# Dealing the depthwise-convolution steps of the last two images evenly over bands, with the convolution's rows at every second SBUF partition

## The chip, the cores and the metric

The kernel runs on one core of one Trainium2 chip. The metric is the device time of one execution in microseconds (us). The kernel before takes 3230.07 us, the median of three runs from 3227.74 to 3243.27 us.

## The reference

The input is a batch of four images of 128 channels and 128 x 128 pixels, float32. Layer 0 cuts each image into 9 x 9 overlapping regions of 16 x 16 pixels (step 14), runs four-head attention with a layer norm in each region, merges the regions, applies a second layer norm and a projection to 256 channels, a depthwise 5 x 5 convolution, a batch norm over the whole batch, GELU twice, a projection back to 128 channels and a residual. Layer 1 is two quantised 3 x 3 convolutions with batch norms. Cut to the part that the change touches:

```python
xf = merged.transpose(0, 2, 3, 1).reshape(b, h * w, c)
y = _ln(xf, ln2_g, ln2_b)
y = y @ w_p0 + b_p0
ym = y.transpose(0, 2, 1).reshape(b, HIDDEN, h, w)          # 256 channels
ym = jax.lax.conv_general_dilated(ym, dw_k, window_strides=(1, 1), padding=[(2, 2), (2, 2)],
        feature_group_count=HIDDEN, dimension_numbers=('NCHW', 'OIHW', 'NCHW'))
mu = ym.mean(axis=(0, 2, 3), keepdims=True)                  # over all four images
```

## The kernel before, in words

**Bands.** The attention part runs over 36 bands, t = 0 to 35: four images of nine bands, each band a row of nine regions. For every region the order on PE, ACT, DVE and SP is the order in which the program is written (a manual schedule); POOL's order is left to the compiler's planner. `beside(t)` (L931) returns, for each of a band's nine regions, the side work that is issued between the attention steps: layer norm and projections of a later band (`ln1_chunks`), the finish of the band before (`post_chunks`), and steps from the list `todo`, mostly steps of the depthwise convolution. `run` (L990) runs a step and then issues the stores it left (`flush`, L440), all on SP.

**Layer norms.** Each band has four layer-norm chunks. A chunk writes its reciprocal deviations to DRAM (`row`, on ACT's queue) and reads them back spread over 128 partitions (`xn<-row`, L420, on SP's queue); DVE's multiply at L430 waits for that.

**The depthwise convolution.** `post_chunks` stores the 256-channel rows to DRAM (`y2_d`, L440) with pixels of even and odd columns apart, in runs of 64 numbers (256 bytes). For images 0 to 2 they lie in [32 rows (16 image rows, even and odd), 256 channels, 9 groups, 64], so that for one row and four channels everything is one run of 8960 bytes. A convolution step loads 32 such rows and 8 halo rows for each of two groups of channels (`half` 0 and 1) into a tile `u`, half 0 at partitions 0 to 39 and half 1 at 64 to 103, and multiplies it with a banded weight tile `w` (`depthwise`, L613, matmuls at L622 of 40 rows by 32 columns). ACT copies the two results to `c` (L690), DVE takes their statistics (L694) and SP stores them to `cv_d`. `conv_steps(n)` (L636) makes these steps: one `begin` and 32 steps for each of images 0 to 2, one `begin` and 16 steps for the first half (rows 0 to 63) of image 3. A step first issues the loads of the step two ahead.

**Loads of a step.** For images 0 to 2 (L656) there are four: for each half the 32 rows and the 8 halo rows, half 0 on SP's queue, half 1 on ACT's. Image 3 has another layout (`input_of`, L628) and its loads are all on SP (L669). Weight tiles are read from `dw_d` (`weights`, L606), two DMAs of 40 partitions by 3 runs of 1 KB, once for two steps (images 0 to 2) or once for each (image 3). `u` and `w` come from a pool of three buffers each, `c` from a pool `cp` of three.

**Dealing.** Steps of image b are put on `todo` when band t = 9(b + 1) + 1 begins and are dealt over nine bands for images 0 and 1 (three or four in a band), over five bands (t = 28 to 32: 6, 7, 7, 7 and 6) for image 2. The first half of image 3 is put there at t = 33 with a divisor of seven: 2, 3 and 3 steps in bands 33 to 35, and nine steps are left for the tail.

**The tail.** After band 35, `beside(T)` finishes the last band's rows with the nine left steps between its pieces (in the tail they use the score banks of PSUM, and their copies are issued one step late, `pending`). Then `conv_rest` (L734) does the second half of image 3 in 16 steps with tiles of its own, `ur` and `wr`, six of each, loaded by SP and POOL (L746, L608); its results go through the same three `c` buffers (L769) and out in two stores for each half (L776, half 0 on SP, half 1 on ACT).

**Preparation.** In bands 0 to 9 `todo` holds the quantisation of two weights and `band_matrices` (L213), which writes zeros around `y2_d` (`edge`, L232, on SP), builds banded weights in DRAM (`band_d`, L254) and turns them into `dw_d`.

After the tail come the GELU stage (L1234) and the two 3 x 3 convolutions.

Of the kernel before, what the change touches and what calls it, by code (L numbers as in the profile page):

```python
# [48 lines left out]
def layers(  # L49
# [44 lines left out]
    cv_d = [dram.tile([P // GR, 2 * P, GR * P], F32, name=f"cv_d{b}") for b in range(B)]  # L94

    dw_d = dram.tile([2 * NCK, KD, 3, 16 * 32], F32, name="dw_d")
# [88 lines left out]
    with ExitStack() as actx:  # L185
# [8 lines left out]
        up, cp = pool("up", 3), pool("cp", 3)  # L194
# [10 lines left out]

        stores = []
        xb, xr, yr, qs, kr, ob = {}, {}, {}, {}, {}, {}

        def scratch(n):

            return up.tile([P, UW], F32, name="u")[:, :n]

        def band_matrices():  # L213
# [18 lines left out]
            def edge(b, m, n, g):  # L232
                if b == B - 1:
                    d = y2_d[b][P + 2 :] if g else y2_d[b][0:2]
                    out = d.rearrange("r e c x -> (r e c x)").rearrange("(p n x) -> p n x", p=P, x=CW)
                else:
                    out = bass.AP(
                        y2_d[b].tensor, y2_d[b][m, 0, g, 0:1].offset,
                        [[n * NG * CW, P], [NG * CW, n], [1, CW]],
                    )  # L240
                nc.sync.dma_start(
                    out=out, in_=held["zero"][:, : n * CW].rearrange("p (n x) -> p n x", x=CW)
                )
# [26 lines left out]
            def turn(c, s, half):  # L270
# [7 lines left out]
                if half:  # L278
                    del held[c, s]
                    nc.sync.dma_start(  # L280
                        out=dw_d[c // 16 : (c + 64) // 16, :, s, :].rearrange("k p n -> p k n"),
                        in_=by_c.rearrange("p (k n) -> p k n", n=16 * 32),
                    )
# [15 lines left out]

            for n, p in enumerate(pieces):  # L300
# [3 lines left out]
                steps.append(lambda p=p: turn(*p, 1))  # L304
            return steps
# [300 lines left out]
        def weights(wt, k, jj, n, dma):  # L606
            for half in range(2):
                dma(  # L608
                    out=wt[64 * half : 64 * half + KD].rearrange("p s c m -> p s (c m)"),
                    in_=dw_d[2 * k + half, :, :, 256 * jj : 256 * (jj + n)],  # L610
                )

        def depthwise(outs, wt, ut, n):  # L613

            for j in range(n // 4):

                for s, (a, z) in ((1, (0, CW)), (0, (1, CW)), (2, (0, CW - 1))):
                    for half in range(2):
                        hs = slice(64 * half, 64 * half + KD)
# [15 lines left out]

        def conv_steps(n, ahead=2):  # L636
# [8 lines left out]
            def load(at):  # L645
                k, jj, c = tiles[at]
                if c == 0:
                    W[k, jj] = up.tile([P, 3, 8, 32], F32, name="w")
                    weights(W[k, jj], k, jj, 1, nc.sync.dma_start)
                if b < B - 1:  # L650
                    t = scratch(UW)
                    U[at] = bass.AP(t.tensor, t.offset, [t.ap[0], [CW, ng], [NG * CW, nc_], [1, CW]])
                    for a, z in ((0, GR), (GR, GR + 4)):
                        for half, engine in enumerate((nc.sync, nc.scalar)):
                            src = y2_d[b][0, 32 * k + 16 * half + 8 * jj + c, 0, 0:1].offset
                            engine.dma_start(  # L656
                                out=t[64 * half + 2 * a : 64 * half + 2 * z],
                                in_=bass.AP(
                                    y2_d[b].tensor, src + (CW if a else 0),
                                    [[2 * P * NG * CW, 2 * (z - a)], [1, UW]],  # L660
                                ),
                            )
# [3 lines left out]
                for half in range(2):  # L666
                    ch = 32 * k + 16 * half + 8 * jj + c
                    for a, z in ((0, GR), (GR, GR + 4)):
                        nc.sync.dma_start(  # L669
                            out=ut[64 * half + 2 * a : 64 * half + 2 * z].rearrange(  # L670
                                "p g c x -> p g (c x)"
                            ),
                            in_=input_of(b, g0, ng, ch, nc_, a, z),
                        )

            def products(at):
                k, jj, c0 = tiles[at]
                ut, wt = U.pop(at), W[k, jj]
                if tail:
                    pc = score_banks(at, ng)  # L680
                else:
                    pc = [ps_m.tile([P, nj, ng, CW], F32, name="pm") for _ in range(2)]
                depthwise(pc, wt[:, :, c0:], ut, nc_)
                return pc

            def results(at, pc):
                k, jj, c0 = tiles[at]
                for half in range(2):
# [4 lines left out]
                    for j in range(nj):  # L693
# [3 lines left out]
                        ch = 32 * k + 16 * half + 8 * jj + c0 + 4 * j  # L697
                        store(
                            bass.AP(
                                cv_d[b].tensor,  # L700
                                cv_d[b][g0, ch, 0:1].offset,
                                [[CW, P], [2 * P * GR * P, ng], [1, CW]],
                            ),
                            cv[:, j],
                        )
# [6 lines left out]
            for at in range(len(tiles)):  # L712
                def one(at=at):
                    if at + ahead < len(tiles):
                        load(at + ahead)
                    while pending:
                        pending.pop(0)()
                    pc = products(at)
                    if tail:
                        pending.append(lambda: results(at, pc))  # L720
                    else:
                        results(at, pc)
# [11 lines left out]
        def conv_rest(n, pool):  # L734
# [8 lines left out]
            def load(at, a, z, g, m):  # L743
                k, jj = tiles[at]
                for half, engine in enumerate((nc.sync, nc.gpsimd)):
                    engine.dma_start(  # L746
                        out=U[at][64 * half + 2 * a : 64 * half + 2 * z, g : g + m].rearrange(
                            "p g c x -> p g (c x)"
                        ),
# [3 lines left out]
            def begin(at):  # L753
                U[at] = pool.tile([P, ng, 8, CW], F32, name="ur", bufs=ahead)
                W[at] = pool.tile([P, 3, 8, 32], F32, name="wr", bufs=ahead)
                weights(W[at], *tiles[at], 1, nc.gpsimd.dma_start)
# [6 lines left out]
            def step(at):  # L763
# [3 lines left out]
                for half in range(2):  # L767
                    cv = cp.tile([P, 2, ng, CW], F32, name="c")
# [3 lines left out]
                    for j in range(2):  # L772
# [3 lines left out]
                        (nc.sync, nc.scalar)[half].dma_start(  # L776
                            out=bass.AP(
                                cv_d[b].tensor,
                                cv_d[b][g0, 32 * k + 16 * half + 8 * jj + 4 * j, 0:1].offset,
                                [[CW, P], [2 * P * GR * P, ng], [1, CW]],  # L780
                            ),
                            in_=cv[:, j],
                        )
# [147 lines left out]
        def beside(t, sel=None):  # L931
# [7 lines left out]
            if t >= 2:  # L939
                b, i = bands[t - 2]  # L940
                if i == NR - 1 and b < B - 1:
                    todo.extend(conv_steps(b))
                    share[0] = NR if b < B - 2 else 5
                elif b == B - 1 and i == 4:
                    todo.extend(conv_steps(B - 1))
                    share[0] = 7
# [3 lines left out]
            conv = [todo.pop(0) for _ in range(n if t < T else 0)]  # L950
# [3 lines left out]
            if t == T:  # L954
                more = lambda n: [todo.pop(0) for _ in range(min(n, len(todo)))]
                return [
                    *more(2), *b1[:2], *b2[:2], b1[2], *more(1), b1[3], b2[2], *more(1), b2[3], b1[4], b2[4],
                    *more(1), b1[5], b2[5], *more(1), b1[6], *b1[7:], b2[6], *more(1), *b2[7:], *more(len(todo)),
# [39 lines left out]
        todo, share, left, early, tail, pending = [], [0], [], [], [], []  # L998
# [14 lines left out]
        with nullcontext() if safe else tc.manual_schedule(engines=MANUAL):  # L1013
# [30 lines left out]
            tail.append(True)  # L1044
# [5 lines left out]
            run(pending)  # L1050
# [183 lines left out]
    def gelu_stage():  # L1234
        with (
# [7 lines left out]
            def load(n):  # L1243
                b, k = units[n]
                cv = ld.tile([P, 2, U], F32, name="cv")
                nc.sync.dma_start(
                    out=cv,
                    in_=cv_d[b][k // 2].rearrange("(h p) n -> p h n", p=P)[:, :, pixels(k % 2)],
                )
# [204 lines left out]
```

## Time and profile before

| | us |
|---|---|
| median of 3 runs | 3230.07 |
| profiled execution | 3225.32 |
| its span, first to last instruction | 3223.5 |
| bands of image 0 (26 to 520) | 494 |
| bands 10 to 18, with the convolution of image 0 | 518 |
| bands 19 to 27, with the convolution of image 1 | 514 |
| bands 28 to 32, with the convolution of image 2 | 351 |
| bands 33 to 35 | 160 |
| tail, first part (2063 to 2165) | 102 |
| tail, `conv_rest` (2165 to 2284) | 119 |

A line of the profile names an engine (PE the matmul engine, DVE, ACT, POOL, and SP, which only issues DMAs), a source line (L622), and a group of instructions with its output and inputs. "xN" is a count. A busy share is time in which an engine works, divided by the stretch. "DMA share" is the mean busy share of the core's 16 DMA engines. PEclk is the share of full speed that PE's clock was granted.

### The profile page before, as it was taken

The page shows a single profiled execution, that of the slowest core. Times are in us where ns is not written, and L with a number is a line of the kernel's source. Part 1 is how long each engine was busy: PE and PEld are TensorE (multiplying, and loading weights), DVE is VectorE, ACT ScalarE, POOL GpSimd, SP SyncE. Part 2 cuts the span into 40 slices and gives each one's busy share as a digit, 9 for nine tenths or more (in the row PEclk, how much of TensorE's full clock was granted, in tenths as well). Part 3 has the DMA queues.
Part 4 walks back from the last instruction along what each step waited for, and adds up shares of the span by engine and source line. Part 5 has one row for each costly group of instructions (what it writes and reads, how often), then busy time and mean ns, then how long its engine had stood idle before and what let it go on. Part 6 is the DMA issues. An engine that isn't in the chain of part 4 may idle for free.

```text
span 3223.5 us, 88862 instructions
## 1 busy us (share of the span) xinstructions
PE 3023.7 (94%) x37626; PEld 1465.0 (45%) x37626; DVE 2009.6 (62%) x3180; ACT 1983.7 (62%) x2642; POOL 876.8 (27%) x1118
## 2 busy tenths in 40 slices
PE   8988999999999999999899999767899999999998
PEld 4544554444444444444444445344444444444443
DVE  5856887777776677767666667512455555666543
ACT  6756786777777677777666667421577777433433
POOL 3433443333333333333233233403111111000000
PEclk9999999999999999999999999865799999999999
DMA  4466666888996889987799987888899999452398
GB/s 87 130 181 187 175 185 170 206 216 207 216 218 164 190 206 214 216 209 194 183 230 226 223 200 187 185 183 171 268 359 358 358 357 298 156 168 74 123 359 303
DMA packets 777118, 688.19 MB, mean 213 GB/s; under 512 B 606206, under 2 KB 655943, under 8 KB 769031
## 3 DMA queue, kind: packets, MB, share of 16 engines
q1 hardware_dynamic: 748263, 634.09, 71.1%
q10 hardware_dynamic: 24160, 39.12, 4.7%
q0 software_dynamic: 4288, 9.19, 1.4%
q8 instruction: 299, 4.90, 0.6%
q14 instruction: 108, 0.88, 0.1%
HBM read 410.68 MB, written 275.51 MB: 213 GB/s over the span
## 4 chain that ended last, share of the span: by engine, by line
PE 74%; DMA 11%; ACT 5%; DVE 4%; issue 3%; SPq 1%; ACTq 1%; POOL 0%; DVEq 0%; POOLq 0%
PE pc L1211 21%; PE pm L447 17%; PE sc L834 8%; PE po L897 8%; PE pm L622 7%; PE pb L1275 7%; DMA cv_d<-c 4%; PE po L905 3%; PE pm L386 3%; DMA y_d<-y 2%; DMA xn<-row 2%; ACT pt L842 2%; DVE rd L917 2%; DMA u<-y_d 1%; PE sc L622 1%
## 5 line engine op out<-in xcount | busy, mean ns | idle before, releaser
L917 DVE RECIPROCAL rd<-po 128x256 f32<-128x256 f32 x324 | 568.6, 1755 | 385.0 <-PE po L905 384.3
L842 ACT ACTIVATE pt<-sc 128x1024 f32<-128x1024 f32 x648 | 628.4, 1025 | 126.9 <-PE sc L834 65.4
L1211 PE MATMUL pc<-q,wq 128*128 128x512 fp8e4 x3168 | 699.4, 381 | 5.1 <-DVE q L1223 5.1
L852 POOL TENSOR_TENSOR sm<-pt 128x512 f32<-128x512 f32 x324 | 415.0, 1281 | 881.6 <-ACT pt L842 611.4
L1211 PEld LDWEIGHTS <-wq 128*128 128x128 fp8e4 x3168 | 308.7, 97 | 406.1 <-issue 37.3
L834 PE MATMUL sc<-q,kr 32*128 32x256 f32 x5184 | 398.5, 403 | 26.8 <-ACT pt L842 26.2
L897 PE MATMUL po<-pt,v 128*32 128x256 f32 x5184 | 353.9, 391 | 30.4 <-DVE part L921 29.3
L834 PEld LDWEIGHTS sc<-q,kr 32*128 32x128 f32 x5184 | 245.4, 184 | 285.4 <-issue 177.0
L622 PE MATMUL pm<-u,w 40*32 40x504 f32 (+3 forms) x5280 | 287.5, 562 | 0.8 <-DMA u<-y_d 0.8
L852 DVE TENSOR_TENSOR sm<-pt 128x512 f32<-128x512 f32 x324 | 244.6, 755 | 33.5 <-ACT pt L842 33.5
L576 ACT ACTIVATE y<-pm,vectors 128x512 f32<-128x512 f32 (+1 forms) x288 | 183.0, 641 | 111.5 <-PE pm L447 55.0
L694 DVE BATCH_NORM_STATS2 st<-c 128x6 f32<-128x512 f32 (+1 forms) x256 | 147.0, 617 | 165.7 <-ACT c L690 165.3
L447 PE MATMUL pm<-xn,wqkv 128*32 128x512 f32 (+1 forms) x2304 | 245.9, 549 | 3.6 <-ACT v L825 2.1
L447 PE MATMUL pm<-xn,wp 128*32 128x512 f32 (+1 forms) x2304 | 242.2, 548 | 5.0 <-DVE rstd L393 1.4
L1275 PE MATMUL pb<-cv,wp 128*128 128x512 f32 x512 | 233.3, 599 | 4.6 <-ACT cv L1266 4.5
L897 PEld LDWEIGHTS po<-pt,v 128*32 128x32 f32 x5184 | 139.0, 110 | 197.2 <-issue 102.4
L690 ACT COPY c<-pm 128x512 f32<-128x512 f32 x206 | 111.4, 591 | 183.7 <-PE pm L622 142.4
L1219 DVE BATCH_NORM_STATS2 st<-pc 128x6 f32<-128x512 f32 x256 | 165.8, 689 | 83.7 <-PE pc L1211 83.7
L905 PE MATMUL po<-sm,ones 128*32 128x256 f32 x2592 | 204.4, 385 | 0.0
L924 POOL TENSOR_TENSOR ob<-ob,part 128x32 f32<-128x32 f32 x288 | 127.7, 443 | 270.2 <-DVE part L921 259.8
L447 PE MATMUL pm<-wqkv,yr 128*32 128x128 f32 x5184 | 179.0, 276 | 0.0
L1283 DVE SCALAR_TENSOR_TENSOR y<-pb,vectors,xfl 128x512 f32<-128x512 f32 x128 | 90.3, 747 | 139.7 <-PE pb L1275 127.4
(161 smaller groups left out, 3590.5 us busy)
## 6 DMA issues: line engine op xcount, KB each, us to landing
cv<-cv_d SPq DMA_DIRECT2D x64, 1024.0 KB
cv_d<-c SPq DMA_DIRECT2D x192, 256.0 KB
xn<-row SPq DMA_DIRECT2D x76, 512.0 KB
y_d<-y SPq DMA_DIRECT2D x142, 256.0 KB
xfl<-xf_d SPq DMA_DIRECT2D x64, 512.0 KB
id_d<-y SPq DMA_DIRECT2D x64, 512.0 KB
idt<-id_d SPq DMA_DIRECT2D x64, 512.0 KB
out_dram<-z SPq DMA_DIRECT2D x64, 512.0 KB
```

The lines of the kernel that those rows point to most:

```text
L447: nc.tensor.matmul(out[m], w[:, m], v, start=True, stop=True)
L576: nc.scalar.activation(y[:, :n], pm[:, : n * P].rearrange("p (r c e) -> p r e c", r=n, e=2), AF.Identity, bias=bp0[:, h : h + 1],)
L622: nc.tensor.matmul(outs[half][32 * q : 32 * q + 32, j, :, a:z], wt[hs, s, c, :], ut[hs, :, c, a + s - 1 : z + s - 1], start=(s == 1), stop ...
L834: nc.tensor.matmul(sc[h // 2][:, h % 2, kc, :].rearrange("p (r c) -> p r c", c=RS), region(kr, j)[hs, kc * P : (kc + 1) * P], queries(j, h ...
L842: nc.scalar.activation(pt, sc[p], AF.Exp)
L852: add(sm, pt[:, :, 0, :], pt[:, :, 1, :], ALU.add)
L897: nc.tensor.matmul(po[hs, 0, :], v[:, kc, hs], pt[h // 2][:, h % 2, kc, :], start=(kc == 0), stop=(kc == 1),)
L905: nc.tensor.matmul(po[hs, 1, :], ones, sm[h // 2][:, h % 2, :], start=True, stop=True)
L917: nc.vector.reciprocal(rd, po[:, 1, :])
L1211: nc.tensor.matmul(pc[:, h], w[:, t, :], q1[b][:, r + dy : r + dy + RB, dx : dx + P], start=(t == 0), stop=(t == 8),)
L1219: nc.vector.bn_stats(st[:, 2 * n + h, :], pc[:, h])
L1275: nc.tensor.matmul(pb[:, m], wp2[:, h, :], cv[:, h, px], start=(h == 0), stop=(h == 1))
```

## The change

- The loads of `u` for images 0 to 2 become two DMAs in place of four: the 32 rows of both halves go in one DMA on SP's queue to the even partitions 0, 2, ... 126, read from DRAM as [2 halves, 32 rows, 8960 bytes]; the 8 halo rows of both go in one DMA on POOL's queue to the partitions 1, 9, ... 121, read as [2, 8, 8960 bytes].
- The loads of `u` for image 3 stay two for each half, the rows on SP's queue (32 even partitions), the halo on POOL's (8 odd ones). `conv_rest` does the same with its own tiles.
- Weights: `dw_d` is laid out anew, so that a tile's row is one run of 3072 bytes, and is read by two DMAs, [2, 32, 3072 bytes] to even partitions and [2, 8, 3072 bytes] to every eighth odd one.
- The matmuls of the convolution read 64 partitions of each half in place of 40. The partitions in between must hold zeros: `u` and `w` become fixed tiles (three of each, taken in turn by `turned`), cleared once by POOL; those of `conv_rest` are cleared in the tail, `ur` by DVE and `wr` by POOL.
- Dealing: in bands 28 to 35 the count is worked out anew, 7, 7, 6, 6, 6, 6, 6 and 6, so that nothing is left for the tail; the parts for steps in the tail (`pending`, `tail`, the score banks in `conv_steps`) are gone.
- Results of image 3: `cv_d` of that image is laid out by groups of four channels, so that one store takes the place of two; `conv_rest` writes to eight result tiles of its own (`cr`) in place of the three shared ones. The GELU stage reads image 3's units with two DMAs in place of one.
- The zeros around `y2_d` are issued by POOL in place of SP; `dw_d` is written by two DMAs in place of one, 24 in place of 12.

```diff
-    cv_d = [dram.tile([P // GR, 2 * P, GR * P], F32, name=f"cv_d{b}") for b in range(B)]
-    dw_d = dram.tile([2 * NCK, KD, 3, 16 * 32], F32, name="dw_d")
+    cv_d = [dram.tile([P // GR, 2 * P, GR * P], F32, name=f"cv_d{b}") for b in range(B - 1)]
+    cv_d.append(dram.tile([2, 2 * P // 4, P // GR // 2, 4, GR * P], F32, name=f"cv_d{B - 1}"))
+    dw_d = dram.tile([2, 2 * NCK, KD, 3 * 8 * 32], F32, name="dw_d")
...
-                nc.sync.dma_start(
+                nc.gpsimd.dma_start(
                     out=out, in_=held["zero"][:, : n * CW].rearrange("p (n x) -> p n x", x=CW)
                 )
...
-        def weights(wt, k, jj, n, dma):
-            for half in range(2):
-                dma(
-                    out=wt[64 * half : 64 * half + KD].rearrange("p s c m -> p s (c m)"),
-                    in_=dw_d[2 * k + half, :, :, 256 * jj : 256 * (jj + n)],
-                )
+        def spread(t, half=None):
+            at, n = (0, P) if half is None else (64 * half, 64)
+            return (slice(0, 2 * GR), t[at : at + n : 2]), (slice(2 * GR, KD), t[at + 1 : at + n : 8])
+
+        def weights(wt, k, jj, dma):
+            flat = wt.rearrange("p s c m -> p (s c m)")
+            for m, out in spread(flat):
+                dma(out=out, in_=dw_d[jj, 2 * k : 2 * k + 2, m])
...
-                        hs = slice(64 * half, 64 * half + KD)
+                        hs = slice(64 * half, 64 * half + 64)
...
-                    for a, z in ((0, GR), (GR, GR + 4)):
-                        for half, engine in enumerate((nc.sync, nc.scalar)):
-                            src = y2_d[b][0, 32 * k + 16 * half + 8 * jj + c, 0, 0:1].offset
-                            engine.dma_start(
-                                out=t[64 * half + 2 * a : 64 * half + 2 * z],
-                                in_=bass.AP(
-                                    y2_d[b].tensor, src + (CW if a else 0),
-                                    [[2 * P * NG * CW, 2 * (z - a)], [1, UW]],
-                                ),
-                            )
+                    src = y2_d[b][0, 32 * k + 8 * jj + c, 0, 0:1].offset
+                    for engine, (m, out) in zip((nc.sync, nc.gpsimd), spread(t)):
+                        engine.dma_start(
+                            out=out,
+                            in_=bass.AP(
+                                y2_d[b].tensor, src + (CW if m.start else 0),
+                                [[16 * NG * CW, 2], [2 * P * NG * CW, m.stop - m.start], [1, UW]],
+                            ),
+                        )
...
-                cv = cp.tile([P, 2, ng, CW], F32, name="c")
+                cv = pool.tile([P, 2, ng, CW], F32, name="cr", bufs=8)
...
-                    share[0] = NR if b < B - 2 else 5
+                    share[0] = NR
                 elif b == B - 1 and i == 4:
                     todo.extend(conv_steps(B - 1))
-                    share[0] = 7
...
-            conv = [todo.pop(0) for _ in range(n if t < T else 0)]
+            if T > t > T - NR:
+                n = -(-(len(todo) + (17 if t < T - 3 else 0)) // (T - t))
+            conv = [todo.pop(0) for _ in range(n)]
```

## The prediction

> **What bounds the kernel now.** First the page's busy times, then the stretches:
>
> ```profile
> PE 3023.7 (94%) x37626; PEld 1465.0 (45%) x37626; DVE 2009.6 (62%) x3180; ACT 1983.7 (62%) x2642; POOL 876.8 (27%) x1118
> ...
> 520.00:1038.00 518.00, 507.04 (x8104) 240.66 (x8096) 363.09 (x563) 370.92 (x561) 188.31 (x239) 0.99 0.83 201
> 1038.00:1552.00 514.00, 503.80 (x8092) 239.23 (x8088) 361.41 (x560) 369.97 (x560) 187.63 (x238) 0.99 0.84 202
> 1552.00:1903.00 351.00, 325.18 (x5180) 149.79 (x5176) 218.13 (x338) 218.68 (x339) 103.81 (x133) 0.99 0.93 219
> 1903.00:2063.00 160.00, 154.97 (x2812) 84.30 (x2808) 113.88 (x188) 112.90 (x166) 57.98 (x71) 0.99 0.73 184
> 2063.00:2165.00 102.00, 59.61 (x1024) 31.73 (x1016) 20.88 (x51) 21.34 (x37) 22.54 (x39) 0.67 0.91 191
> 2165.00:2284.00 119.00, 85.37 (x1536) 60.27 (x1536) 32.45 (x126) 17.66 (x32) 25.21 (x42) 0.50 0.76 157
> ```
>
> The columns of a stretch are its length, busy PE, PEld, DVE, ACT and POOL, granted clock, DMA share and GB/s. In the bands PE is busy 92 to 98%: they are bound by PE. Bands 5 to 9, without convolution, take 46.5 us each by the first score matmuls of bands 5 and 10 (287.1, 519.6). Bands 10 to 18 carry 33 steps, (518 - 9 x 46.5) / 33 = 3.0 us each; bands 28 to 32 also 33, (351 - 232.5) / 33 = 3.6, with DMA at 0.93. The tail has PE at 58 and 72%, and the waits say why:
>
> ```profile
> ACT c L690 <- DMA cv_d<-c: 75.0, 14, 33.7
> POOL ur L746 <- DMA y_d<-y: 69.7, 1, 69.7
> ACT c L769 <- DMA cv_d<-c: 61.3, 12, 7.3
> ```
>
> Columns: total us, times, longest. The three result buffers come free only when a store has landed, and the last loads of `conv_rest` wait for the last rows. So the tail has time to give, and DMA, not PE, is what the bands run into next. How do DMAs spread over the 16 engines? SP's queue in the preparation:
>
> ```profile
> 211.14 6.82 SPq L254 DMA_DIRECT2D band_d<-pad_d  x2
> ...
> 219.64 8.19 SPq L254 DMA_DIRECT2D band_d<-pad_d  x2
> ```
>
> Columns: start, duration. These copies are described as [3, 20, 2048 bytes]. From 165 to 325 us the trace's DMA records have their 2048-byte packets running exactly three at a time in 66% of the time in which any runs. The loads of `u` on ACT's queue, described as [32, 8960 bytes], reach 16 at a time. The outermost count, not the size, decides.
>
> [...] The fastest twentieth of the 8960-byte packets takes 338 ns, 26.5 GB/s[...]; their mean from 520 to 1038 us is 579 ns.
>
> **The change part by part.**
>
> *Loads of images 0 to 2.* The new row load has 64 destination partitions, but its source is [2, 32, 8960 bytes]: the outermost count is 2, and the new weight load's [2, 32, 3072 bytes] too. [...] Cost on each of the two: 32 packets x 338 ns = 10.8 us a step, where the old shares were 80 packets / 16 x 338 ns = 1.7 us on average. Weights: (64 + 16) / 2 packets x 119 ns (the fastest twentieth of the 3072-byte packets before) = 4.8 us for two steps. The halo, [2, 8], goes by POOL[...]: 16 x 338 / 16 = 0.3 us on average.
>
> Everything else is spread and still has to pass these two engines. By the packet records, without the `u` and weight loads, each engine carries 318 us in bands 10 to 18 (236 if every packet took its size's fastest twentieth) and 220 (158) in bands 28 to 32; I let bands 19 to 27 stand as 10 to 18. Added for one image: 32 x 10.8 + 16 x 4.8 + 11 = 434 us.
>
> - Image 0: 236 to 318 + 434 = 670 to 752 us on the two engines, against 518 that the bands take now: +152 to +234.
> - Image 1: 670 to 752 against 514: +156 to +238.
> - Image 2: 592 to 654 against 351: +241 to +303. The new dealing gives bands 28 to 32 32 steps for 33, so no relief.
>
> Sum +549 to +775. It is a floor: it needs the two engines busy without a break. [...] Serially, a step adds 10.8 + 2.4 + some 4 of other traffic - 6 of slack = 11 us: 96 x 11 = 1056. I take 790, near the floor's upper end, because in a saturated stretch the stall is also the time in which the engines work.
>
> *Bands 33 to 35* get 18 entries for 8, and the nine steps at 3.0 us each cost +27. Image 3's row loads are [32, 4, 2048 bytes] and run on 16 engines. But its weights, 4.8 us a step x 16 = 77 us, add to at most 108 us of other traffic and some 30 of new loads and stores: 215 against 187. I add +15: +42.
>
> *The tail.* The first part loses the nine steps. What is left is a chain: POOL's seams, projection, squares, variance, two activations, spreading, multiply, eight projections and copies, store: from the rows 2.2 + 3.6 + 1.1 + 2.2 + 1.5 + 2 x 2.1 + 2.6 + 7.3 us, with gaps some 30, and 10 for landing and loads. DVE's clearing of six `ur` tiles stands before it: 0.17 us for 128 columns (L1155) scales to at most 2.7 us for 2048, 16 us in all, of which half is hidden by POOL and PE. 48 us for 102: -54. In `conv_rest` the wait for `c` goes (eight tiles for three). A step takes 119 / 16 = 7.4 us now; at half clock PE needs 5.4:
>
> ```profile
> 2040.55 2.79 PE L622 MATMUL pm<-u,w 40*32 40x256 f32 x96
> ...
> 2220.39 5.42 PE L622 MATMUL sc<-ur,wr 40*32 40x256 f32 x96 [1.02 <-ACT c L769]
> ```
>
> and DMA 0.76 x 7.4 = 5.6. With 6.2 a step, 99: -20. [...] Sum -74.
>
> *Smaller edits.* Matmuls over 64 rows for 40: at nothing, as a matmul's time follows its columns (128 rows by 256 columns take 391 ns, 32 by 256 403). POOL issues 128 more halo loads at 0.57 us (the row of L746): 73 us, hidden in its 882 us of idle before `sm`; uncovered they would cost at most 73, below nothing they cannot be. The zeros on POOL: [...] between -15 (bands 3 and 4 take 58 and 62 us for 46.5, with SP held at L254) and +30; I take -5. Clearing, 24 `dw_d` writes and 16 more loads in the GELU stage: single issues of 0.3 us, at nothing.
>
> Sum: 790 + 42 - 74 - 5 = +753, against the span of 3223.5, with 1.8 us around it: 3225.3 + 753 = 3978. The median of the runs lies 5 us above the profiled execution. As the floor gives 3225.3 + 549 + 42 - 74 - 5 = 3737, I shade a little towards it and say **3930 us**.
>
> **Rivals.**
>
> *The loads are spread after all* (chance 0.07). If the issuing engine divides by the 64 partitions and not by the 2, the row load takes 64 x 338 / 16 = 1.4 us, and nothing is lost in the bands: 27 - 74 - 5 = -52, 3173 us. [...] against it, the three at a time. Where it decides: an image's loads need 2 x (346 + 77) / k = 846 / k us beside the halo's 11; image 0 has 518 - 318 = 200 to spare, image 2 351 - 220 = 131, so k = 8 would do and k = 4 would not.
>
> *Spread, but POOL stalls* (0.05). A halo load on POOL that waits for a tile holds `sm` behind it, and PE waits for `sm`. POOL idles some 2.7 us before each `sm` (882 / 324). If each of 128 halo loads in the bands waits 4 us beyond its issue, 128 x (4 - 2.7) = +166: 3340 us. Against it: the tile was released a step before.
>
> *Two engines, and no overlap* (0.23 of the two-engine case's 0.88): the serial 1056 in place of 790, 4245 us. [...]
>
> **How the numbers follow.** Two engines 0.88, spread 0.07, POOL 0.05. Within the first, from 3690 (below the floor, for gains missed) to 4250: about 0.78 of all. The range 3640 to 4270 holds 0.8; the other cases lie outside it below. A measurement of this kernel can't tell less than 0.5%, 16 us, from no change. Faster 0.06 (nearly all of spread), same 0.02, slower 0.92.
>
> **What the profile after would show.** Bands of images 0 and 1 at 70 us and more, those of image 2 above 110; PE below 75% busy there; 8960-byte packets on SP's queue two at a time; waits of DVE for `xn<-row`, of ACT for `y` stores and of PE for `u` in the hundreds of us; a mean DMA share below 0.7 in spite of it; the tail near 150 us, without waits of copies for `cv_d` stores. Wrong would be: bands of 57 us, or 8960-byte packets 16 at a time (then the spread rival), or `sm` waiting on POOL's queue (then the second).

## The result, and the profile after

The changed kernel takes 3941.51 us (3938.23 to 3949.66) against 3229.86 us (3227.74 to 3243.27): a ratio of 1.2196 [1.2159, 1.2234]. Its profiled execution took 3949.66 us, its span 3947.8. The ratio of each experiment below is to runs of the kernel before made beside it; their medians lie between 3230 and 3245 us.

First the busy times and the chain that ended last, from the page of the kernel after:

```profile
PE 3161.4 (80%) x37626; PEld 1483.1 (38%) x37626; DVE 2029.7 (51%) x3186; ACT 1984.4 (50%) x2642; POOL 970.3 (25%) x1269
...
PE 43%; DMA 38%; ACT 6%; SPq 5%; DVE 5%; issue 3%; ACTq 0%; POOL 0%; DVEq 0%; POOLq 0%
DMA cv_d<-c 26%; PE pc L1221 17%; PE pm L466 8%; PE pb L1291 5%; DMA y_d<-y 4%; PE sc L845 4%; PE po L908 3%; PE pm L644 3%; DMA xn<-row 3%; ACT pt L853 2%; DMA u<-y_d 2%; SPq L459 2%; SPq L479 2%; DVE rd L928 2%; PE po L916 1%
```

PE executes the same 37626 matmuls but is busy 80% of the span for 94%. DMAs make up 38% of the chain, and most of that is one transfer, the store of a convolution result (`cv_d<-c`, 26%). That store is not one of the loads whose shape the change altered.

Now the stretches of the kernel after, with the same columns as before (length, busy PE, PEld, DVE, ACT, POOL, granted clock, DMA share, GB/s): bands 0 to 9, 10 to 18, 19 to 27, 28 to 32, 33 to 35, the tail's first part, and `conv_rest` up to the GELU stage.

```profile
30.00:508.00 478.00, 450.46 (x7080) 239.57 (x7076) 384.34 (x585) 358.34 (x530) 222.64 (x270) 0.98 0.62 167
508.00:1269.00 761.00, 557.83 (x8120) 249.68 (x8112) 363.93 (x561) 371.19 (x563) 209.62 (x274) 0.86 0.47 137
1269.00:2018.00 749.00, 554.55 (x8096) 247.69 (x8092) 360.84 (x559) 369.55 (x560) 205.16 (x270) 0.87 0.48 138
2018.00:2635.00 617.00, 381.78 (x5148) 164.72 (x5136) 221.14 (x338) 219.42 (x338) 121.30 (x165) 0.80 0.42 122
2635.00:2865.00 230.00, 188.04 (x3492) 102.59 (x3496) 121.31 (x213) 115.11 (x175) 73.57 (x101) 0.90 0.68 169
2865.00:2922.00 57.00, 32.76 (x352) 12.45 (x352) 25.31 (x33) 17.56 (x29) 25.22 (x42) 0.77 0.84 209
2922.00:3014.00 92.00, 61.14 (x1548) 49.18 (x1532) 36.48 (x150) 18.20 (x33) 31.59 (x60) 0.78 0.97 222
```

The bands with loads of images 0 to 2 grew from 518, 514 and 351 us to 761, 749 and 617, while the mean share of the 16 DMA engines fell from 0.83, 0.84 and 0.93 to 0.47, 0.48 and 0.42. Longer, with idler DMA engines on average: the picture of a few engines that are full while the rest wait. PE's own work also grew, from 507 to 558 us in the first of them at a granted clock of 0.86 for 0.99, but that leaves PE idle for 203 of 761 us. In the packet records the 8960-byte packets of SP's queue run exactly two at a time in 90% of the time in which any runs; before there were up to 16. The stretches without such loads, bands 0 to 9 and the tail, became shorter.

How full are the two engines? The records give an estimate: the time of all packets but those of the row and weight loads, divided by 16, plus the time of these loads, divided by two. With the loads' packets at their fastest twentieth (338 and 119 ns) or at their mean in this run, it comes to 726 to 756 us for the 761 of the first stretch, 724 to 754 for 749 and 624 to 651 for 617. (754 for 749 shows how rough the estimate is.) So the two work practically without a break. The records do not name the engine of a packet; that it is the same two every time is inferred from this sum, as with changing pairs each engine would have had 361, 358 and 258 us to do.

All stages side by side, each measured from the first exponentials of its bands (so a stretch can differ from the rounded windows by some us):

| | before | after | difference |
|---|---|---|---|
| bands 0 to 9 | 493.3 | 478.4 | -15 |
| bands 10 to 18 (loads of image 0) | 518.5 | 760.6 | +242 |
| bands 19 to 27 (image 1) | 514.0 | 748.9 | +235 |
| bands 28 to 32 (image 2) | 351.3 | 617.4 | +266 |
| bands 33 to 35 (image 3) | 149.0 | 230.3 | +81 |
| from there to the first GELU (tail) | 236 | 149 | -87 |
| rest, with the GELU stage | 933 | 933 | 0 |

The waits of the kernel after that a late DMA ended (total us, times, longest):

```profile
ACT c L713 <- DMA cv_d<-c: 527.3, 76, 15.3
ACT y L595 <- DMA y_d<-y: 234.4, 85, 14.6
DVE xn L449 <- DMA xn<-row: 134.4, 42, 22.9
PE pm L644 <- DMA u<-y_d: 63.0, 12, 14.9
```

The loads of `u` themselves are hardly waited for: they are issued two steps ahead. Who waits, by this reading, is whatever else goes through the same two engines with less lead: first the copies into the three `c` tiles, whose stores have to land first, then `y`, then `xn`. The largest of these waits was 75 us before, 62 of it in the tail.

### The profile page after: what moved, and what is told of

It is laid out like the page before. It is cut to its first block, busy times and chain, and to the rows that moved or that the text cites. A ratio compares the mean times of both kernels' runs of the same rounds, so it can differ in the third digit from the quotient of the medians.

```text
span 3947.8 us, 88649 instructions
## 1 busy us (share of the span) xinstructions
PE 3161.4 (80%) x37626; PEld 1483.1 (38%) x37626; DVE 2029.7 (51%) x3186; ACT 1984.4 (50%) x2642; POOL 970.3 (25%) x1269
## 4 chain that ended last, share of the span: by engine, by line
PE 43%; DMA 38%; ACT 6%; SPq 5%; DVE 5%; issue 3%; ACTq 0%; POOL 0%; DVEq 0%; POOLq 0%
DMA cv_d<-c 26%; PE pc L1221 17%; PE pm L466 8%; PE pb L1291 5%; DMA y_d<-y 4%; PE sc L845 4%; PE po L908 3%; PE pm L644 3%; DMA xn<-row 3%; ACT pt L853 2%; DMA u<-y_d 2%; SPq L459 2%; SPq L479 2%; DVE rd L928 2%; PE po L916 1%
## 5 line engine op out<-in xcount | busy, mean ns | idle before, releaser
L853 ACT ACTIVATE pt<-sc 128x1024 f32<-128x1024 f32 x648 | 628.2, 1024 | 119.2 <-PE sc L845 65.8
L713 ACT COPY c<-pm 128x512 f32<-128x512 f32 x224 | 128.3, 588 | 795.5 <-DMA cv_d<-c 527.3
L466 PE MATMUL pm<-xn,wp 128*32 128x512 f32 (+1 forms) x2304 | 303.7, 648 | 269.1 <-ACT c L713 136.3
L845 PE MATMUL sc<-q,kr 32*128 32x256 f32 x5184 | 415.1, 421 | 71.5 <-ACT pt L853 71.4
L644 PE MATMUL pm<-u,w 64*32 64x504 f32 (+3 forms) x6144 | 339.1, 564 | 95.8 <-DMA u<-y_d 63.0
L845 PEld LDWEIGHTS sc<-q,kr 32*128 32x128 f32 x5184 | 255.4, 193 | 346.8 <-issue 196.4
L908 PE MATMUL po<-pt,v 128*32 128x256 f32 x5184 | 362.8, 399 | 19.6 <-DVE part L932 19.0
L405 PE MATMUL pm<-sq,ones 128*32 128x256 f32 (+1 forms) x1152 | 100.3, 419 | 242.0 <-ACT sq L399 242.0
L466 PE MATMUL pm<-xn,wqkv 128*32 128x512 f32 (+1 forms) x2304 | 264.9, 587 | 7.5 <-ACT v L836 6.8
L466 PEld LDWEIGHTS pm<-xn,wp 128*32 128x32 f32 x2304 | 70.7, 121 | 434.6 <-ACT c L713 154.3
L644 PEld LDWEIGHTS pm<-u,w 64*32 64x32 f32 x6144 | 113.4, 110 | 277.8 <-issue 208.2
```

The lines of the kernel that those rows point to most:

```text
L466: nc.tensor.matmul(out[m], w[:, m], v, start=True, stop=True)
L644: nc.tensor.matmul(outs[half][32 * q : 32 * q + 32, j, :, a:z], wt[hs, s, c, :], ut[hs, :, c, a + s - 1 : z + s - 1], start=(s == 1), stop ...
L845: nc.tensor.matmul(sc[h // 2][:, h % 2, kc, :].rearrange("p (r c) -> p r c", c=RS), region(kr, j)[hs, kc * P : (kc + 1) * P], queries(j, h ...
L853: nc.scalar.activation(pt, sc[p], AF.Exp)
L908: nc.tensor.matmul(po[hs, 0, :], v[:, kc, hs], pt[h // 2][:, h % 2, kc, :], start=(kc == 0), stop=(kc == 1),)
```

## The experiments

**The loads cut in two, all else as after.** If two engines are the whole loss, one DMA for each half of the loads, with 32 partitions as its outermost count, takes it away and leaves the gains.

```diff
-            for m, out in spread(flat):
-                dma(out=out, in_=dw_d[jj, 2 * k : 2 * k + 2, m])
+            for half in range(2):
+                for m, out in spread(flat, half):
+                    dma(out=out, in_=dw_d[jj, 2 * k + half, m])
...
-                                [[16 * NG * CW, 2], [2 * P * NG * CW, m.stop - m.start], [1, UW]],
+                                [[2 * P * NG * CW, m.stop - m.start], [1, UW]],
```

> The changed kernel with every load whose source began with the two halves cut into one DMA for each half, on the same queues: rows [32, 8960 bytes] and [32, 3072 bytes], halos [8, ...]. Nothing else differs. Two engines as the cause: bands 10 to 18 and 19 to 27 return to 505 to 525 us each, bands 28 to 32 to 340 to 360, and only the tail, the preparation and the dealing remain: 3225 - 15 (preparation, as the changed kernel shows) + 42 - 88 = 3165 us, between 3130 and 3200. Loads on POOL as the cause (halos behind POOL's other work): they are still there, more of them, so it stays above 3700 us.

Measured: 3131.96 us, 0.9656 [0.962, 0.9693] of before. The DMA issues of the kernel after, and then of this one (count, size of one):

```profile
u<-y_d SPq DMA_DIRECT2D x96, 560.0 KB
```

```profile
u<-y_d SPq DMA_DIRECT2D x192, 280.0 KB
```

The same bytes in twice as many DMAs; the 8960-byte packets again run up to 16 at a time. And the stretches of bands 10 to 35 of this kernel (columns as above):

```profile
507.00:1030.00 523.00, 508.78 (x8116) 240.70 (x8112) 366.30 (x561) 371.63 (x562) 225.74 (x306) 0.99 0.79 200
1030.00:1546.00 516.00, 504.96 (x8092) 239.37 (x8088) 365.04 (x559) 369.96 (x560) 220.88 (x302) 0.99 0.80 201
1546.00:1888.00 342.00, 325.87 (x5152) 149.62 (x5146) 219.67 (x337) 219.47 (x339) 137.94 (x197) 0.98 0.91 222
1888.00:2070.00 182.00, 172.29 (x3492) 96.63 (x3487) 120.64 (x213) 114.76 (x174) 73.51 (x101) 0.97 0.85 211
```

PE is busy 97, 98 and 95% in the first three. So the whole of +743 us in the bands of images 0 to 2 hangs on the shape in which the row, halo and weight loads are described. This kernel is faster than both others: 3.4% faster than the kernel before.

**The shape alone, in the kernel before.** Only the row loads of images 0 to 2 are described anew there, with 2, 4 or 8 as the outermost count; sizes, queues and number of DMAs stay. The rows land in another order, so the convolution of these images computes other numbers.

```diff
-                                    [[2 * P * NG * CW, 2 * (z - a)], [1, UW]],
+                                    [[2 * P * NG * CW, 2 * (z - a)], [1, UW]] if a else
+                                    [[2 * P * NG * CW, 2], [2 * 2 * P * NG * CW, 16], [1, UW]],
```

(4 and 8 likewise, with 8 and 4 inside.)

> The kernel before, with one thing changed: the source of each 32-row load of images 0 to 2 is described as [2, 16, 8960 bytes] in place of [32, 8960 bytes], with the same bytes, packets, queues and partitions (the rows lie in another order in the tile, so the convolution's numbers are not the reference's). Two engines as the cause: each of them gets 346 us of rows an image; with 318 + 20 (weights) + 11 that is 695 us for 518 and 514, and 220 + 18 + 346 + 11 = 595 for 351, so some +177 + 181 + 244 = +600 us: 3830, between 3690 and 3950. If the slowdown comes from anything else in the change (POOL's loads, the order of the tiles, 64-row matmuls), this stays within 1% of 3230.

> As the run with two, but the source is described as [4, 8, 8960 bytes]: four engines, 173 us of rows an image on each. Two-engine arithmetic: 318 + 20 + 173 + 11 = 522 for 518 and 514, nothing to +10 each, and 220 + 18 + 173 + 11 = 422 for 351, +71: some +85 us, 3315, between 3250 and 3400. [...]

> As the runs with two and four, but the source is described as [8, 4, 8960 bytes], so eight engines (rows of the tile in another order, the convolution's numbers are not the reference's). Two-engine arithmetic with the four-engine run's surcharge: 318 + 20 + 87 + 11 = 436 for 518 and 514, nothing; 220 + 18 + 87 + 11 = 336 for 351, at the limit, 0 to +20: 3230 to 3265 us. If the outermost count cost something by itself[...], it would stay as far up as the run with four, some 200 us.

| outermost count | us | ratio | bands 10-18, 19-27, 28-32 |
|---|---|---|---|
| 32 (before) | 3241.12 | 1 | 518, 514, 351 |
| 8 | 3256.20 | 1.0028 [1.0011, 1.0046] | 517, 510, 367 |
| 4 | 3458.06 | 1.0668 [1.0616, 1.0721] | 580, 578, 451 |
| 2 | 3891.56 | 1.2006 [1.1949, 1.2062] | 721, 721, 597 |

(The run with 8 was compared with 3245.42 us.) Apart from the order of the rows nothing but this number differs, and it gives the loss in order of its size. With 2, SP's 8960-byte packets run two at a time in 69% of the time in which any runs, with 4 four at a time in 46%, with 8 eight at a time in 29%, each time the most frequent number. The outermost count, and with it the number of packets at a time, is shown as the cause. The rows alone, with 2, cost 656 us in these bands, where the whole change cost 743. The stretches of bands 10 to 32 with 2, and then with 4, are:

```profile
529.00:1250.00 721.00, 589.03 (x8112) 257.66 (x8112) 367.37 (x562) 370.95 (x562) 187.21 (x238) 0.87 0.54 145
1250.00:1971.00 721.00, 573.81 (x8092) 252.57 (x8088) 363.32 (x559) 368.74 (x560) 187.60 (x238) 0.88 0.54 144
1971.00:2568.00 597.00, 397.16 (x5180) 176.30 (x5176) 220.82 (x338) 220.69 (x339) 103.43 (x133) 0.79 0.48 128
```

```profile
528.00:1108.00 580.00, 527.04 (x8104) 244.55 (x8104) 363.25 (x562) 369.91 (x561) 187.64 (x239) 0.95 0.70 180
1108.00:1686.00 578.00, 524.53 (x8096) 244.42 (x8092) 360.52 (x559) 369.87 (x561) 187.67 (x238) 0.96 0.69 179
1686.00:2137.00 451.00, 366.90 (x5184) 162.76 (x5177) 218.86 (x338) 220.29 (x340) 103.72 (x133) 0.88 0.66 171
```

The run with 4 missed its expectation (3250 to 3400 us) on the high side. The sum of busy times, which fits with 2, gave next to no loss for bands 10 to 27 with 4, and they lost 62 and 64 us. The sum had 522 us for 518, with the rows at the fastest packets' 338 ns; in the run the 8960-byte packets took 375 ns on SP's queue and 499 on ACT's (bands 10 to 18). By the estimate from the run's own records, as above, the four engines have 530 to 597 us to do there.

**Another queue for the row loads.** If the capacity of two engines is the bound, another queue changes nothing; if what hurts is that stores are issued on SP right behind a row load, the loads on ACT's queue would free them, and the time would fall to the prediction's floor, 3737 us, or below.

```diff
-                    for engine, (m, out) in zip((nc.sync, nc.gpsimd), spread(t)):
+                    for engine, (m, out) in zip((nc.scalar, nc.gpsimd), spread(t)):
```

> The changed kernel with the two-engine row loads of images 0 to 2 issued on ACT's queue in place of SP's[...]. Capacity of the two engines as the bound: they carry the same work, so it stays at 3900 to 3980 us. [...]

Measured: 3961.66 us, 1.2222 [1.2164, 1.228]. No gain. Its waits (columns as above):

```profile
DVE xn L449 <- DMA xn<-row: 412.9, 73, 32.0
ACT c L713 <- DMA cv_d<-c: 409.2, 54, 21.0
```

Together 822 us, where the kernel after has 662 in these two; the wait of ACT for the stores of `y` fell from 234 to 106. The row loads do not hold ACT itself: they take 0.53 us each to issue (0.72 at most). The waits were dealt out anew, and the bands take 751, 764 and 625 us: which queue the loads are on changed who waits, and how long the bands take hardly changed (761, 749 and 617 with the loads on SP's), as the capacity of two engines would have it.

**Rows spread, weights still on two engines.** How much of the loss is the weights'?

```diff
-            for half in range(2):
-                for m, out in spread(flat, half):
-                    dma(out=out, in_=dw_d[jj, 2 * k + half, m])
+            for m, out in spread(flat):
+                dma(out=out, in_=dw_d[jj, 2 * k : 2 * k + 2, m])
```

(against the kernel with all loads cut in two)

> The changed kernel with only the u loads of images 0 to 2 cut by half; the weight loads still begin with [2, ...] and run on two engines. Arithmetic: 318 + 54 (rows) + 77 (weights) + 11 = 460 for 518, no loss; 220 + 54 + 77 + 11 = 362 for 351, 0 to +20; bands 33 to 35 as in the changed kernel, 230 us against 182 with spread loads, +48; conv_rest 79 against 70, +9. Together +57 to +77 on 3132: 3190 to 3210 us. If weights on two engines cost nothing, 3132.

Measured: 3302.87 us, 1.0191 [1.0139, 1.0242]. A second miss on the same side. The stretches of bands 10 to 35:

```profile
504.00:1053.00 549.00, 516.72 (x8116) 242.05 (x8116) 365.72 (x562) 371.77 (x563) 227.07 (x308) 0.98 0.77 190
1053.00:1593.00 540.00, 512.23 (x8084) 239.40 (x8082) 362.10 (x559) 369.28 (x560) 220.94 (x302) 0.98 0.77 192
1593.00:1987.00 394.00, 340.99 (x5168) 158.12 (x5168) 219.82 (x337) 220.33 (x339) 137.40 (x197) 0.93 0.79 191
1987.00:2219.00 232.00, 187.88 (x3496) 102.07 (x3488) 122.88 (x213) 115.23 (x175) 73.36 (x101) 0.90 0.69 168
```

The first stretch is 26 us longer than with all loads spread (548.6 against 522.8); the others are 24, 52 and 50 us longer, and the part from the end of the bands to the GELU stage 17. The 3 KB rows of the weights on two engines cost some 170 us in all. The expected sum, 460 us for the first stretch and 362 for that of image 2, priced the spread rows and halos at the fastest packets, 54 us (and then the halos once more, 11), but at their mean durations in this run (638 and 578 ns) they take each engine 100 us in the first stretch. By the estimate from the run's own records the two engines have 484 to 518 us to do in the first stretch and 374 to 408 in that of image 2. Bands 33 to 35 stand at 232 us as in the kernel after (230), so their excess there is the weights'; in these bands of the kernel after, the 3072-byte packets of SP's queue run two at a time in 72% of the time in which any runs.

**The other parts alone, in the kernel before.** The dealing (7 to 6 steps in each of the last eight bands), the eight result tiles of `conv_rest`, and both:

```diff
-                    share[0] = NR if b < B - 2 else 5
+                    share[0] = NR
...
-                    share[0] = 7
...
+            if T > t > T - NR:
+                n = -(-(len(todo) + (17 if t < T - 3 else 0)) // (T - t))
```

> The kernel before with the new dealing alone: 7, 7, 6, 6, 6, 6, 6, 6 entries in bands 28 to 35 and none in the tail. Bands 33 to 35: 149 to 179 us (nine steps at 3.0 and some contention). Tail, first part: 102 to 48. conv_rest as it was, 119, since it keeps its three result tiles. -24 us: ratio 0.992, between 0.986 and 0.998. If the tail's steps only filled time in which PE waited for the chain anyway, the tail gives nothing back and it is slower by 27 us: 1.008.

```diff
-                    cv = cp.tile([P, 2, ng, CW], F32, name="c")
+                    cv = pool.tile([P, 2, ng, CW], F32, name="cr", bufs=8)
```

> The kernel before with eight result tiles of its own in conv_rest in place of the three shared ones, and nothing else. The wait of ACT's copies for cv_d stores in conv_rest (61 us) goes; a step falls from 7.4 to some 6.2 us, the DMA work: -20 us, ratio 0.994. If DMA is the bound of conv_rest already, nothing: 1.000.

> Both together: -24 - 20 = -44 us, ratio 0.986. The changed kernel with spread loads stands at 0.966, 3132 us. If this reaches it within 10 us, the even partitions and the merged stores gave nothing beyond what the tail and the dealing give; what is missing to it, about 60 us by this estimate, belongs to them and to the zeros moved to POOL (15).

| | us | ratio | bands 33-35 | tail, first part | `conv_rest` |
|---|---|---|---|---|---|
| before | 3245.42 | 1 | 149 | 116 | 112 |
| dealing | 3217.72 | 0.9922 [0.9893, 0.9951] | 201 | 52 | 105 |
| result tiles | 3219.36 | 0.9925 [0.9899, 0.995] | 151 | 119 | 82 |
| both | 3207.89 | 0.9889 [0.9863, 0.9915] | 201 | 52 | 87 |

(The columns of parts are each kernel's profiled execution; the tail's first part is counted from the last exponentials to the first matmul of `conv_rest`.) The dealing moves work: 64 us leave the tail and 52 come back in bands 33 to 35, where 30 were expected. The two parts together gain 38 us, less than their sum of 54: `conv_rest` gains 30 from the tiles in the kernel before and 18 after the dealing. With three result tiles the waits of `conv_rest` are still there after the dealing. From the profile of the kernel with the dealing alone, over its tail:

```profile
DVE st L773 <- ACT c L769: 96.3, 19, 28.7
ACT c L769 <- DMA cv_d<-c: 48.5, 10, 7.9
```

and with eight tiles, in the tail of the kernel after:

```profile
DVE st L788 <- ACT cr L784: 69.1, 14, 25.7
...
ACT cr L784 <- DMA cv_d<-cr: 18.0, 5, 5.7
```

**Everything but the even partitions.** Dealing, result tiles, merged stores of image 3 and the zeros on POOL, with loads, weights and matmuls at the old 40 partitions. Beside the two parts above:

```diff
-                nc.sync.dma_start(
+                nc.gpsimd.dma_start(
                     out=out, in_=held["zero"][:, : n * CW].rearrange("p (n x) -> p n x", x=CW)
...
+    cv_d.append(dram.tile([2, 2 * P // 4, P // GR // 2, 4, GR * P], F32, name=f"cv_d{B - 1}"))
...
-                        store(
-                            bass.AP(
...
+                    store(result_of(b, g0, ng, 32 * k + 16 * half + 8 * jj + c0, nj), cv.rearrange("p j g x -> p (j g) x"))
```

> The kernel before with the dealing, the tail's own tiles, the merged stores of image 3 and the zeros on POOL, but with the rows where they were: partitions 0 to 39 and 64 to 103, four loads a step on SP and ACT, weights in runs of 1 KB, matmuls of 40 rows. Against the kernel with spread loads (0.966) it lacks only the even partitions and what they bring. The zeros gave -22 us there (bands 0 to 9: 478 for 500), the merged stores should give some -10 in conv_rest and -10 in bands 33 to 35: 0.9889 - 42 / 3240 = 0.976, between 0.970 and 0.982. At 0.966 the even partitions are worth nothing; at 0.989 they are worth all.

Measured: 3178.98 us, 0.9817 [0.9768, 0.9866]. Bands 0 to 9 fall from 501 us (with dealing and result tiles) to 479, which is the zeros' doing; `conv_rest` takes 88 us for 87, so one store in place of two bought nothing there. What is left between this kernel and the 0.9656 of the one with the loads cut in two is the new layout: 64 partitions, weights in runs of 3072 bytes, rows all on SP's queue and halos on POOL's. Bands 28 to 32 go from 355 to 341 us, bands 33 to 35 from 196 to 182, `conv_rest` from 88 to 70. Which part of it does this was not told apart.

**Clearing on POOL.** With the loads cut in two, the `ur` tiles of `conv_rest` are cleared by POOL in place of DVE, where they stand between the last bands and the chain of the tail:

```diff
-                for t, engine in zip(ring[-1], (nc.vector, nc.gpsimd)):
-                    engine.memset(t, 0.0)
+                for t in ring[-1]:
+                    nc.gpsimd.memset(t, 0.0)
```

> The kernel with spread loads, and the six ur tiles of the tail cleared by POOL in place of DVE. In the chain of the spread kernel DVE's six clearings stand one behind the other from 2082 to 2095 us, 12.9 us, before the first projection of the tail. With them on POOL the stretch from the last band to conv_rest's first matmul falls from 52 to some 42 us: -10 us, ratio 0.9625. If POOL, which has six weight tiles to clear and 24 loads to issue there, becomes late instead, nothing: 0.9655.

Measured: 3132.81 us, 0.9656 [0.9615, 0.9696], the same as without. In the kernel with the loads cut in two, DVE clears (min, median, max in ns):

```profile
L773 DVE MEMSET ur<- x6: 1765/1765/1765, 2082.2 to 2093.0; 128x2048 f32 x6
```

So 10.6 us of DVE, which POOL then does no sooner: the last of the six is clear at 2098.5 us, with DVE at 2094.7, and the first part of the tail took 54.5 us for 51.9.

## Why the prediction was right

*Two engines, 790 us.* Right in mechanism, a little high in size. For a count of two the kernel before had the three at a time of [3, 20, 2048 bytes] to show; in the kernel after SP's 8960-byte packets, the rows, run two at a time in 90% of the time, and POOL's, the halos, in 80%. That the two are the same for every load was the author's estimate, and so was a sixteenth of the halos' time for each engine; only the sum of the result section bears on the first, and no run on the second. Measured are +242, +235 and +266, +743 in all, at or near the upper ends that the sum of busy times gave for the images (+234, +238, +303). That it was a floor, to be exceeded, was wrong: the upper sums, with the other traffic at its mean of before and the new loads at 338 and 119 ns, are the time itself for images 0 and 1, and 37 us too much for image 2. The 338 ns held: the packets of the row loads took 345 to 347 ns on average, and no 8960-byte packet of any run took less than 335 ns, 26.7 GB/s. What the prediction said of the stall, that it "is also the time in which the engines work", holds by the estimate of the result section (726 to 756 us of work in 761). Bands of 84, 83 and 123 us with PE busy 73, 74 and 62% came as it said.

*The total, 3930.* That it lies within 12 us of the measured 3941.51 is in part luck. The sum of the terms was 3978; 790 was 47 too high, bands 33 to 35 were 39 too low, the gains 23 too small, and 48 were taken off only because the floor lay lower.

*No overlap (4245 us).* Fell: the two engines work through the waits, and 8960-byte packets ran two at a time in 90% of their time. The 4 us of other traffic and 6 of slack in its 11 us a step were the author's estimate. *Spread after all (3173).* Fell with the packets. Its boundary, "k = 8 would do and k = 4 would not" (k engines for a row load), held with the rows alone: 1.003 and 1.067. *POOL stalls (3340).* Fell: `sm` waits 1077 us, but for ACT's exponentials. Before its halo loads POOL does wait for PE, 122 us in all, but the waits of others for `sm` add up to 6 us. With all loads cut in two the halo loads, then twice as many, stayed on POOL without harm.

*Who waits.* Here the prediction named the wrong head, DVE's waits for `xn<-row` and ACT's for the stores of `y`. Both are there, with 134 and 234 us, but the largest wait, 527 us, is ACT's copies for the three `c` tiles. Their stores are issued on SP right behind a row load, as the timeline of SP's queue from 2308 us (in the bands of image 2) of the kernel after shows (start, duration):

```profile
2308.12 0.51 SPq L688 DMA_DIRECT2D u<-y_d  x1
2308.72 12.86 SPq L459 DMA_DIRECT2D cv_d<-c  x2
2321.68 4.25 SPq L479 DMA_DIRECT2D xt<-in_x_dram  x1
```

That a store waits there because of the row load ahead of it was not shown: with the row loads on ACT's queue the copies still wait 409 us. Of PE for `u` it said "in the hundreds", and it is 63: these loads are issued two steps ahead. Whether more than three `c` tiles would shorten these waits was not tried.

*Bands 33 to 35, +42.* Undersized: +81. The nine steps, taken as +27 at 3.0 us each, cost +52 with the dealing alone in the kernel before and +33 with the new layout (182.4 against 149.0). The other 48 are the weights on two engines (230.3 against 182.4). For them the prediction's own sum had 215 us of work for 187, which is +28, and it took +15 without giving a reason. By the estimate from the packet records of the kernel after, the two engines have 221 to 246 us to do in the 230. The row loads of image 3, [32, 4, 2048 bytes], are spread there as predicted: the 2048-byte packets of SP's queue run up to 16 at a time.

*The tail, -74.* Measured -87. The first part gained 60, taken as 54 (the dealing alone gained 64 in the kernel before), and `conv_rest` 33, taken as 20; some 5 came back between its last matmul and the first GELU. The copies' waits for `cv_d` stores did not go altogether: 18 us are left there. The clearing was sized at no more than 2.7 us a tile and is 1.77.

*The zeros on POOL, -5.* Measured -15 in bands 0 to 9, and -22 when they are moved in a kernel that is otherwise as before in this stretch. The profiled execution of the kernel before is the shortest there of those with the zeros on SP: 493 us, where the six others take 499 to 501. So the effect is at or below the lower end of the range, -15 to +30; the upper end was the author's estimate, with no measurement behind it. *The rest at nothing.* The matmuls over 64 partitions have the median that they had over 40, 582 for 583 ns. POOL's halo loads take 0.57 us each; all that others wait for POOL's `sm` behind them is the 6 us above.

The terms as measured: 743 + 81 - 87 - 15 = +722 us; the profiled executions differ by 3949.66 - 3225.32 = +724.

## What to carry to other kernels

When two DMAs are merged by adding a dimension in front, look at the new outermost count. With 2, 4 and 8 in front, packets ran mostly two, four and eight at a time in this kernel (69, 46 and 29% of the time), and with 3 three at a time (66%). With two loads of [32, ...] merged into one of [2, 32, ...] it became 22% slower than before, and with the same bytes in two DMAs 3.4% faster. A mean DMA share of 0.42 to 0.48 beside 527 us of waits for stores was no room to spare here, and another queue didn't help (1.2222 for 1.2196). The sum of work priced the two engines well: its upper ends were +234, +238 and +303, the measured +242, +235 and +266. Near saturation the answer hung on the price of a packet: the fastest packets, 338 ns, made the sums of two experiments too low, and durations beside other traffic (375 and 499 ns with four engines, 638 and 578 with the weights on two) came nearer.

## What the runs showed of the hardware that was not expected

*How full an engine may be.* The estimate of the result section, made for the runs in which few engines carry more than the rest (in us). For halos of [8, ...] it divides by eight, as rows with 8 in front ran eight at a time most often (29%), and for the old weights of [40, ...] by ten: in the kernel before their 1024-byte packets run ten at a time in 13% of the time, the most frequent number above one.

| few engines carry | bands | their work, estimate | stretch with the loads spread | measured |
|---|---|---|---|---|
| rows, eight engines | 10 to 18 | 442 to 481 | 518 | 517 |
| rows, eight engines | 28 to 32 | 337 to 375 | 351 | 367 |
| weights, two engines | 10 to 18 | 484 to 518 | 523 | 549 |
| weights, two engines | 28 to 32 | 374 to 408 | 342 | 394 |
| rows, four engines | 10 to 18 | 530 to 597 | 518 | 580 |
| rows, four engines | 28 to 32 | 426 to 490 | 351 | 451 |

At 85 to 93% of the stretch nothing is lost, at 93 to 99% 26 us are. Above that the measured time lies within the estimate. The packet times are those of each run, longer beside other traffic (638 ns for a row packet in the run with the weights on two engines, 338 at the fastest), so this is a measure made afterwards, not a forecast. Where below a full engine the loss begins no run shows; stretches that no edit touched differ by some 5 us from run to run.

*The issues take longer too.* The issues of result stores on SP's queue, from band 10 to 32 (min, median, max in ns), in the kernel before, in the one after, and with the loads cut in two:

```profile
L440 SPq DMA_DIRECT2D cv_d<-c x190: 359/391/2353, 567.5 to 1895.2; - x190
```

```profile
L459 SPq DMA_DIRECT2D cv_d<-c x188: 354/1340/16206, 567.0 to 2618.3; - x188
```

```profile
L459 SPq DMA_DIRECT2D cv_d<-c x189: 361/533/2505, 551.1 to 1887.9; - x189
```

An issue of such a store takes up to 16.2 us where it took 2.4 at most. All DMA instructions on SP in these bands add up to 1710 us in the kernel after, 656 before and 716 with the loads cut in two. SP issues in the order of the program: in the timeline above the two stores take SP from 2308.72 to 2321.58 us, and a load of `x` follows at 2321.68. With the row loads on ACT's queue SP's still add up to 1403 us, and one store takes up to 21.9 us to issue, though of the loads on two engines only the weights' are left on SP. What makes an issue wait was not shown.
